# Loading x of four tiles in transfers of uneven row counts, in a kernel bound by its stores

## The chip, the cores and the metric

The kernel runs on one core of one Trainium2 chip. The metric is device time in microseconds (us), lower is better. The kernel before took 1336.84 us (median of 3 runs, 1336.64 to 1336.99). A ratio is the mean time of one kernel's fast runs over that of the other's of the same rounds, so it is not quite the ratio of the medians that are quoted beside it; the interval behind it is 95%. "Faster" and "slower" mean by more than 2%.

## The reference

```python
# r_inputs: (4096, 32, 64) float32; W: (496, 64, 64) float32, one matrix for each pair i < j of the 32 fields
i_idx, j_idx = np.triu_indices(32, k=1)
vdotw = einsum('bpd,pde->bpe', inputs[:, i_idx, :], W)
out = (vdotw * inputs[:, j_idx, :]).reshape(4096, 496 * 64)
```

The output has 4096 x 31744 floats, 520 MB, and must be written once. The inputs are 42 MB.

## The kernel before

The 4096 batch rows are 32 tiles of 128. TensorE transposes x of a tile and multiplies it by W (which stays in SBUF); VectorE multiplies the products in PSUM by x and writes them into a ring in SBUF; each tile leaves in four stores on SyncE's queue. x has three slots in SBUF and comes on ScalarE's queue, two tiles to a load.

```python
STORES = [[0, 1], [2, 3], [4, 5, 6], [7, 8, 9, 10, 11, 12, 13, 14, 15]]
RING = 28160                                   # floats per partition, for the stores' data
# x_slots: loads [0], [1,2], [4,3], [5,6], [8,7], ... two tiles each, three slots
    def load_x(load):
        at = sum(len(before) for before in x_loads[: x_loads.index(load)]) * P * F * D
        n = len(load) * F * D
        s = load[0][1]
        nc.scalar.dma_start(                   # 128 rows of 16384 bytes for two tiles
            out=xbuf[:, s * F * D : s * F * D + n],
            in_=x[at : at + P * n].rearrange("(p c) -> p c", p=P),
        )
# ...
    for t in range(NT):
        for load in x_loads:
            if min(load)[0] == t + 1:
                load_x(load)                   # a tile ahead
        for s, group in enumerate(STORES):
            if at + store_w[s] > RING:
                at = 0
            osb = ring[:, at : at + store_w[s]]
            # ... transposes, matmuls, and VectorE's products into osb ...
            nc.sync.dma_start(
                out=out[:, t * cols + o0 : t * cols + o0 + store_w[s]], in_=osb
            )
```

## Time and profile before

| | before |
|---|---|
| median time | 1336.84 us |
| span of the core in the profile, granted TensorE clock | 1335.1 us, 0.962 |
| TensorE, VectorE busy | 87%, 89% |
| VectorE's waits for stores | 102.6 us in 44 waits |
| moved | 562.87 MB at 422 GB/s |

The prediction below shows the busy shares, the DMA queues and the waits. These lines of the same page complete them: bytes, the summary of the chain of work that ended last, and two lines of the DMA issues (count, KB each, median us from issue to landing).

```profile
HBM read 41.94 MB, written 520.09 MB: 421 GB/s over the span
...
DMA 47%; DVE 38%; issue 9%; PE 5%; DVEq 0%; ACT 0%
...
out_dram<-ring SPq DMA_DIRECT2D x32, 4896.0 KB, 17.7
...
x<-in_x_dram ACTq DMA_DIRECT2D x15, 2048.0 KB, 20.4
```

The chain of last work is nearly half transfers, and the transfers are stores: 520 of the 562 MB. Everything that VectorE finishes has to find room in the ring, and room comes when a store has landed on the last of its DMA engines: the one issued at 418.46 landed at 436.7 on the median engine and at 440.28 on the last, and VectorE went on at 440.37. x is a small part of the traffic, but its rows pass through the same engines (from 419.4 us the fast ones have 1448 ns of store, 611 ns of x, and so on in turn), and it is these rows that the change hands out unevenly.

### The profile page before, as it was taken

To read this page: it belongs to the slowest core of one execution; us is meant where nothing else is said; L and a number is where in the kernel's file an instruction comes from. 1 tells how busy PE (TensorE), PEld (TensorE's weight loads), DVE (VectorE), ACT (ScalarE), POOL (GpSimd) and SP (SyncE) were. 2 spreads that over 40 slices of the span, in tenths; PEclk is the share of its full clock that TensorE was granted. 3 is DMA by queue.
4 is the path that set the end of the run, shared out by engine and by line. 5 is a ranking of instruction groups with operands and counts; after the bars stand their busy time and mean duration, and the time that the engine had idled before them with its cause. 6 is when DMAs were issued, how large, how long until landed. Compare 5 with 4: busy or idle time off the path is not lost.

```text
span 1335.1 us, 13080 instructions
## 1 busy us (share of the span) xinstructions
PE 1160.6 (87%) x5376; PEld 544.9 (41%) x5376; DVE 1183.4 (89%) x1376; ACT 66.1 (5%) x65; POOL 0.7 (0%) x6
## 2 busy tenths in 40 slices
PE   6998989989899898998989889798998979989893
PEld 3443334443344443444444444344443434354441
DVE  5998989989899898998989899898998989989894
ACT  0000000000000000000000000000000000000000
POOL 0000000000000000000000000000000000000000
PEclk9999999989899999998989999899999999989997
DMA  9999999999999999999999999999999999999998
GB/s 397 433 430 430 431 428 430 418 433 430 413 425 410 436 414 427 426 414 433 405 432 431 419 429 411 432 426 421 428 413 430 426 407 417 429 421 423 429 425 352
DMA packets 21659, 562.87 MB, mean 422 GB/s; under 512 B 2400, under 2 KB 2400, under 8 KB 2656
## 3 DMA queue, kind: packets, MB, share of 16 engines
q1 hardware_dynamic: 19152, 528.49, 92.8%
q10 hardware_dynamic: 2448, 33.56, 5.9%
q8 instruction: 42, 0.69, 0.2%
q14 instruction: 17, 0.14, 0.0%
HBM read 41.94 MB, written 520.09 MB: 421 GB/s over the span
## 4 chain that ended last, share of the span: by engine, by line
DMA 47%; DVE 38%; issue 9%; PE 5%; DVEq 0%; ACT 0%
DMA out_dram<-ring 46%; DVE ring L180 32%; DVE ring L188 5%; PE pring L170 5%; DMA x<-in_x_dram 1%; DVEq L180 0%; PE pring L130 0%; ACT xT L131 0%; DVEq L225 0%; DVEq L188 0%
## 5 line engine op out<-in xcount | busy, mean ns | idle before, releaser
L170 PE MATMUL pring<-w,xT 64*128 64x512 f32 (+4 forms) x4864 | 1098.4, 564 | 146.4 <-DVE ring L180 133.5
L180 DVE TENSOR_TENSOR ring<-pring,x 128x1024 f32<-128x1024 f32 (+3 forms) x1056 | 1104.1, 1108 | 131.4 <-DMA out_dram<-ring 102.6
L170 PEld LDWEIGHTS pring<-w,xT 64*128 64x128 f32 x4864 | 489.3, 191 | 711.7 <-DVE ring L180 533.0
L131 ACT COPY xT<-pring 128x1024 f32<-128x1024 f32 x64 | 64.8, 1012 | 1224.1 <-PE pring L130 1224.1
L188 DVE TENSOR_TENSOR ring<-pring,x 128x64 f32<-128x64 f32 (+3 forms) x320 | 97.7, 356 | 2.6 <-DMA out_dram<-ring 1.9
L130 PEld LDWEIGHTS pring<-ident,x 128*128 128x128 f32 x512 | 55.6, 142 | 58.8 <-DVE ring L180 50.2
L130 PE MATMUL pring<-ident,x 128*128 128x128 f32 x512 | 70.8, 282 | 8.6 <-DMA x<-in_x_dram 8.6
L131 ACT ACT_TABLE_LOAD x1 | 1.3, 1283 | 1.7 <-PEq L221 1.7
masks.py:199 POOL TENSOR_SCALAR_AFFINE_SELECT ident<-ident 128x128 f32<-128x128 f32 x1 | 0.3, 292 | 0.1
masks.py:197 POOL MEMSET ident<- 128x128 f32 x1 | 0.2, 204 | 0.3 <-POOLq L221 0.3
L221 POOL MEMSET const-bfloat16-1.0<- 128x1 bf16 x1 | 0.1, 101 | 0.0
L221 POOL MEMSET const-uint8-127<- 128x1 uint8 x1 | 0.1, 101 | 0.0
L221 POOL MEMSET const-float32-0.0<- 128x1 f32 x1 | 0.1, 98 | 0.2 <-issue 0.2
L221 POOL MEMSET const-float32-1.0<- 128x1 f32 x1 | 0.1, 98 | 0.0
## 6 DMA issues: line engine op xcount, KB each, us to landing
out_dram<-ring SPq DMA_DIRECT2D x32, 4896.0 KB, 17.7
out_dram<-ring SPq DMA_DIRECT2D x32, 3936.0 KB, 18.1
out_dram<-ring SPq DMA_DIRECT2D x32, 3776.0 KB, 18.3
out_dram<-ring SPq DMA_DIRECT2D x32, 3264.0 KB, 18.6
x<-in_x_dram ACTq DMA_DIRECT2D x15, 2048.0 KB, 20.4
w<-in_w_dram SPq DMA_DIRECT2D x1, 2592.0 KB, 28.1
x<-in_x_dram ACTq DMA_DIRECT2D x2, 1024.0 KB, 12.8
w<-in_w_dram SPq DMA_DIRECT2D x1, 2016.0 KB, 22.2
```

Source lines behind the costliest of these rows:

```text
L130: nc.tensor.transpose(pt[:, ts(c, P)], xt[:, ts(n * g + c, P)], ident)
L131: nc.scalar.copy(xT[:, ts(g, 2 * BANK)], pt)
L170: nc.tensor.matmul(pm[:, h * BANK : h * BANK + n], xT[h * D : (h + 1) * D, ts(p, P)], w_sb[h * D : (h + 1) * D, a : a + n], start=True, st ...
L180: nc.vector.tensor_tensor(runs(osb, o[0], o[1], n), runs(pm, 0, BANK, n), bass.AP(xj.tensor, xj.offset, [xj.ap[0], [0, 2], xj.ap[1]]), ALU ...
L188: nc.vector.tensor_tensor(osb[:, o[h] + h * D : o[h] + n], pm[:, h * (BANK + D) : h * BANK + n], xj[:, h * D :], ALU.mult,)
L221: nc = bacc.Bacc("TRN2", target_bir_lowering=False, num_devices=1)
```

## The change

Its intent, as described with it: 112 rows of x of four tiles come by the lowest seven DMA engines, so that the others are relieved. Each of the four loads concerned is issued per tile, and the tile named in `PART_LOADED` in five pieces of 16, 49, 49, 7 and 7 rows.

```diff
+PART_LOADED = [4, 12, 20, 28]
+ROWS = [slice(0, 16), slice(16, 65), slice(65, 114), slice(114, 121), slice(121, 128)]
...
-        nc.scalar.dma_start(
-            out=xbuf[:, s * F * D : s * F * D + n],
-            in_=x[at : at + P * n].rearrange("(p c) -> p c", p=P),
-        )
+        dst = xbuf[:, s * F * D : s * F * D + n]
+        src = x[at : at + P * n].rearrange("(p c) -> p c", p=P)
+        if not any(t in PART_LOADED for t, _ in load):
+            nc.scalar.dma_start(out=dst, in_=src)
+            return
+        for k, (t, _) in enumerate(load):
+            c = ts(k, F * D)
+            for r in ROWS if t in PART_LOADED else [slice(0, P)]:
+                nc.scalar.dma_start(out=dst[r, c], in_=src[r, c])
```

## The prediction

> **What bounds the kernel now.** I read the page's busy shares first, then the DMA queues, the waits, and the chain of work in one load period. The first lines:
>
> ```profile
> PE 1160.6 (87%) x5376; PEld 544.9 (41%) x5376; DVE 1183.4 (89%) x1376; ACT 66.1 (5%) x65; POOL 0.7 (0%) x6
> ...
> DMA  9999999999999999999999999999999999999998
> ...
> q1 hardware_dynamic: 19152, 528.49, 92.8%
> q10 hardware_dynamic: 2448, 33.56, 5.9%
> ```
>
> VectorE is busy 89% of the span of 1335.1 us, so it is not the limit. The packets of the four DMA queues add up to 92.8 + 5.9 + 0.2 = 98.9% of sixteen DMA engines' span (q1 carries the stores and w, q10 carries x). Sixteen equal engines at 98.9% would leave 1.1%, some 14.7 us, and that caps what balancing can bring, unless packets get quicker. The waits agree: VectorE's long waits are for stores that have not landed and whose ring space it wants.
>
> ```profile
> DVE ring L180 <- DMA out_dram<-ring: 102.6, 44, 6.2
> ```
>
> The share of sixteen hides which engine it is. Each transfer has sixteen landings in the trace, one an engine. I took them for all 128 stores. After 330 us the picture is the same everywhere: some twelve to fourteen land within 0.2 us of each other, one or two are up to 2 us late (mean of the second last: 1.6 us after the median), and one is 3.5 to 6.5 us late (mean of the last there: 4.3 us). It was 2.0 us on average in the first 165 us, then about 4. So one engine is behind the others all the time, and a store is finished when that one is.
>
> The packet records have no engine number, but a packet starts 3 or 4 ns before its predecessor on the engine ends, so they can be chained into engines. The chain that lands last has all its 133 + 17 transfers, 1329 us of packets after taking off the overlaps, and only 2.1 us in gaps over 60 ns. It is simply full. Its packets are longer: 992, 1142, 1199 and 1481 ns (medians for the 26112, 30208, 31488 and 39168 byte rows of a store), against 968, 1119, 1166 and 1448 ns in the chains of others. Eight rows of each a tile make 8 x (24 + 23 + 33 + 33) = 0.9 us a tile, 29 us in 32 tiles. Three chains of other engines, which came out complete, have 1313 us of packets, 8 of these in 39168-byte packets that were stretched (mean 1483 against 1448) just after a pause, and 14 to 15 us of gaps. They have 20 us or so to spare; the full one has nothing.
>
> Where the others pause is seen at a load, here the one of tiles 12 and 11, in two-microsecond windows (the last two columns are the share of sixteen DMA engines and GB/s):
>
> ```profile
> 415.00:417.00 2.00, 1.77 (x11) 1.18 (x12) 2.00 (x3) 0.00 (x0) 0.00 (x0) 1.00 1.14 488
> 417.00:419.00 2.00, 2.00 (x11) 1.43 (x11) 2.00 (x7) 0.00 (x0) 0.00 (x0) 1.00 0.23 99
> 419.00:421.00 2.00, 2.00 (x14) 1.34 (x12) 2.00 (x3) 0.00 (x0) 0.00 (x0) 1.00 1.03 325
> ```
>
> At 417.8 the fast engines run dry until the next store, issued at 418.46, reaches them at 419.37. The slow engine still works on the store before it until 423.1. The chain there:
>
> ```profile
> 418.46 21.82 DMA out_dram<-ring
> 440.28 0.03 issue
> ...
> 461.66 17.18 DMA out_dram<-ring
> ```
>
> That store lands at 440.28 on the slow engine (436.7 on the median one), VectorE gets its space and goes on at 440.37, and the next store of this kind is issued at 461.66. Here too the slow engine has work left, until 466.4. So it has 4 to 5 us in hand whenever the others starve: it never idles, and its own sum of packets is the time.
>
> [...] The trace agrees that exactly one engine is slow, and cannot say its number. [...] an engine alternates between its queues packet by packet. The trace agrees: from 419.4 us a fast engine does 1448 ns of store, 611 ns of x, 1448, 611, eight times.
>
> **The change part by part.** A normal load gives each engine eight rows of a tile. With 16, 49, 49, 7 and 7 rows, engines 0 to 6 get 1 + 7 + 7 + 1 + 1 = 17 rows and engines 7 to 15 get 1. The four loads concerned bring two tiles each. Before, a row of both tiles was one packet of 16384 bytes; after, it is two of 8192 bytes, as in the first and the last load (309 ns, against 611).
>
> - The slow engine, if it is among 7 to 15: removed 8 x 616 ns = 4.93 us (its mean for 16384 bytes); added 9 packets (8 of the normal tile, 1 of the other) x 311 ns = 2.80 us. Minus 2.13 us a load, minus 8.5 us in four. It lies on the path whole, since that engine has no gap.
> - Engines 0 to 6: 25 x 309 = 7.73 us in place of 8 x 611 = 4.89: plus 2.84 us a load, plus 11.4 us in four. They have about 20 us to spare, so it lies beside other work, as long as they don't fall behind the slow one by much. At a load after 330 us they are 3.7 us or more ahead; the shift between them is 2.84 + 2.13 = 4.97, so they come out about 1 us behind it, and are ahead again after one or two tiles at 0.9 us a tile. At the first load, of tiles 4 and 3 near 91 us, the slow engine is only 1.6 us behind, and engines 0 to 6 come out some 3 us behind it. They then set when space comes free, within the 4 to 5 us that the slow one has in hand. I allow 0.7 us for what of this shows.
> - Issues: five more on ScalarE's queue, at 0.37 us each some 2 us, four times. ScalarE is 5% busy and its next copy is 13 us later: nothing.
> - Semaphore writes are packets of 9 ns: nothing.
>
> Sum: 1336.84 - 8.5 + 0.7 = 1329.0 us.
>
> **The order of the two tiles, the step I doubted most.** In each of these loads the part-loaded tile (4, 12, 20, 28) goes out before its mate (3, 11, 19, 27), which is needed first. On engines 0 to 6 the mate's rows stand behind 17 packets, and each waits for a store's packet. If all were issued at 418.46, the 25th packet would come after eight rounds of 1448 + 309, eight of 1119 + 309 and eight of 968 + 309 ns, 35.7 us, and land at about 456; tile 11 is first transposed at 451.3. But the old single load waited for the later of two slots. ScalarE reaches it early:
>
> ```profile
> 409.15 1.01 ACT L131 COPY xT<-pring 128x1024 f32<-128x1024 f32 x1 [18.09 <-PE pring L130]
> 418.46 0.37 ACTq L106 DMA_DIRECT2D x<-in_x_dram  x1
> ```
>
> Tile 12's slot was tile 8's, done with some 40 us earlier, so its five transfers can go at 410. Eight of the 17 packets then travel with the store in flight and fill the pause at 417.8, eight with the next, and the mate's eight follow with the one after it: landing at about 447, some 4 us before it is needed (2 us if VectorE runs 2 us ahead). At 745.9 and 1074.1 us the gap from load to transpose is as long (33.0 and 33.8 us).
>
> [...]
>
> **The rivals.**
> - A: the mate's late x stalls TensorE, because the transfers don't go early. Against it: the two slots are tracked apart, for VectorE works on the third slot while a load is in flight. It would hold the store at 461.66 back by some 3 to 5 us, starve all engines, and eat the 2.1 us a load or more: 1336 to 1340.
> - B: the slow engine is among 0 to 6. Then it gets plus 2.84 us four times: 1336.84 + 11.4 = 1348. For it: no record has the number. Against it: [...] that the change was aimed this way. I give it 5%.
> - C: the spare time of engines 0 to 6 isn't usable where it is wanted (most of it lies after 250 us, in pauses), or their rows, which go to other engines' partitions, take longer than 309 ns. Then part of the 8.5 us is lost: 1330 to 1335.
>
> **Range and chances.** The gain can hardly exceed 8.5 us plus noise of 0.3 us or so[...]. So 1326.5 at the lower end. C and part of A make the upper end 1335. No mechanism here makes 2% (26.7 us): even balance without loss gives 14.7, and B costs 11.4.
>
> **What would show it right or wrong.** Right: mean DMA share still about 99% over a span 7 to 9 us shorter; VectorE's waits for stores shorter; the pause at 417 to 419 smaller; the last landing of a store less late behind the median just after each of the four loads by 2 to 3 us, with seven engines now late with it; no wait of TensorE for x beyond the first, of 8.6 us. Wrong: TensorE's transposes waiting for x in tiles 2, 10, 18 and 26 (A); stores after the four loads landing 3 us later than before, with one engine nearly 8 us behind (B); x rows of over 309 ns on a queue (C).

## The result and the profile after

The changed kernel took 1348.39 us (1348.32 to 1348.65, 6 runs) against 1336.90 us of the kernel before in the same rounds: ratio 1.0086 (1.0073 to 1.0099), "same" by the 2% rule, but 11.5 us longer where 7.8 us less were predicted. The results are correct.

The page of the changed kernel, first the lines that answer to the prediction's first ones (busy shares, DMA share in 40 slices, queues with packets, MB and share of sixteen engines), then the wait of VectorE for the stores (us in total, times, longest) and that of TensorE for x:

```profile
PE 1165.1 (87%) x5376; PEld 556.1 (41%) x5376; DVE 1183.7 (88%) x1376; ACT 66.1 (5%) x65; POOL 0.7 (0%) x6
...
DMA  9999999999998999999999999999999999999998
...
q1 hardware_dynamic: 19152, 528.49, 92.1%
q10 hardware_dynamic: 3136, 33.56, 5.9%
```

```profile
DVE ring L190 <- DMA out_dram<-ring: 108.0, 47, 6.2
...
PE pring L140 <- DMA x<-in_x_dram: 8.7, 1, 8.7
```

VectorE works as long as before (1183.7 against 1183.4 us). The DMA shares of the queues fell to 92.1 + 5.9 + 0.2 = 98.2%, over a span of 1346.5 us, which is 1322 us of packets for a mean engine; before it was 98.9% of 1335.1, or 1320 us. So the engines together do the same work, and nearly all of the longer span is idle time of some of them: balance got worse. TensorE never waits for x except at the very start, as before (8.6 us there). The granted clock in these two profiles, 0.962 and 0.953, is no cause: a longer run told below had 0.960.

Where it happens is seen at a load. The chain of work around tile 12's load, kernel after (start, length):

```profile
382.27 20.25 DMA out_dram<-ring
402.52 0.03 issue
...
411.72 20.63 DMA out_dram<-ring
432.35 0.03 issue
```

And the timeline of ScalarE there:

```profile
382.27 4.00 ACTq L119 DMA_DIRECT2D x<-in_x_dram  x5
393.32 1.01 ACT L141 COPY xT<-pring 128x1024 f32<-128x1024 f32 x1 [19.14 <-PE pring L140]
416.59 1.01 ACT L141 COPY xT<-pring 128x1024 f32<-128x1024 f32 x1 [22.26 <-PE pring L140]
426.31 0.38 ACTq L119 DMA_DIRECT2D x<-in_x_dram  x1
```

The five pieces go at 382.27, as soon as tile 8 has been read for the last time, and the mate, tile 11, alone at 426.31. The pieces go earlier than at the 410 of the prediction, so the mate did not stand behind them: it had landed on all engines by 443.1, and the first transpose of it came at 457.1.

For each transfer the trace has its landings, one an engine: sixteen, and seven for a 49-row piece. Each line gives those of one transfer in us after their median, in order (worked out from the trace, not a view):

```
49 rows, issued at 382.7:  -0.71 -0.66 -0.38  0.00  0.06  0.08  2.43
49 rows, issued at 383.0:  -0.70 -0.69 -0.38  0.00  0.03  0.09  2.43
store, issued at 391.1, the last eight:  0.04  3.90  3.91  4.23  4.59  4.63  4.68  8.68
store, issued at 398.5, the last seven:        3.61  3.66  3.96  4.32  4.36  4.40  8.30
store, issued at 426.3, the last four:   0.04  0.06  0.07  4.17
for comparison, before, store of 428.5, the last two:  1.72  3.66
```

Seven engines come late behind the others after the pieces, as they should. One of the seven is later than the other six by 4 us, which is just the distance at which the slow engine is always behind (4.17 two stores later, when the six have caught up). And one of the seven is already 2.4 us late with the 49-row pieces themselves. This speaks for a slow engine among the seven, to which the change gave rows instead of taking them; the chains of packets below show it.

Two-microsecond windows of before and after, where the engines other than the late ones run dry (third busy column: VectorE; last two columns: share of sixteen DMA engines, GB/s). Before, from 421 on, two microseconds after its pause at 417 to 419:

```profile
421.00:423.00 2.00, 2.00 (x12) 0.80 (x10) 1.82 (x2) 0.00 (x0) 0.00 (x0) 1.00 1.00 432
423.00:425.00 2.00, 1.00 (x5) 0.17 (x4) 0.70 (x1) 0.00 (x0) 0.00 (x0) 1.00 1.05 453
```

After:

```profile
411.00:413.00 2.00, 1.76 (x8) 0.30 (x4) 0.69 (x1) 0.00 (x0) 0.00 (x0) 1.00 1.04 435
413.00:415.00 2.00, 0.71 (x4) 0.30 (x4) 0.99 (x2) 0.00 (x0) 0.00 (x0) 1.00 0.92 393
...
421.00:423.00 2.00, 2.00 (x10) 0.87 (x12) 1.87 (x4) 0.00 (x0) 0.00 (x0) 1.00 0.52 220
423.00:425.00 2.00, 1.77 (x11) 1.03 (x10) 2.00 (x4) 0.00 (x0) 0.00 (x0) 1.00 0.44 189
425.00:427.00 2.00, 2.00 (x11) 1.56 (x11) 2.00 (x6) 0.00 (x0) 0.00 (x0) 1.00 0.30 130
```

Before, the pause at 417 to 419 (share 0.23, shown in the prediction) costs a mean engine 0.77 x 2 = 1.5 us, and by 421 all are busy. After, the six microseconds from 421 cost it (0.48 + 0.56 + 0.70) x 2 = 3.5 us. VectorE is busy in them; its wait lies before, at 411 to 415, where it stands 2.3 us until 414.0 for ring space, because the store of 391.1 landed on its last engine only at 413.9. So its next store is ready only at 426.3, and the engines that are done have nothing to move until then. The slow engine can't make up what it has lost, since it works through the pauses of the others already (before, its 1329 us of packets had 2.1 us of gaps).

The chains of packets say it too. Chained as in the prediction, exactly one chain of the kernel after has longer store packets than the rest (22 to 33 ns more in the median, by row size), and that chain has 241 packets of the x queue. An engine among the lowest seven should have 11 x 8 + 2 x 8 + 4 x (17 + 8) = 204 rows of x and one semaphore write for each of its 11 + 2 + 4 x 6 = 37 transfers, so 241; one of the other nine should have 88 + 16 + 4 x (1 + 8) = 140 rows and one write for each of its 11 + 2 + 4 x 2 = 21 transfers, so 161. The sum fits the page: 7 x 241 + 9 x 161 = 3136, the packets of q10; and the page's packets under 512 B, the semaphore writes, are 2576 against 2400 before, 176 more, as four times 60 in place of 16 should be. The slow chain is one of the seven.

The DMA issues of the kernel after, as a check that the pieces are what they should be (count, KB each, and for the second the median us to landing):

```profile
x<-in_x_dram ACTq DMA_DIRECT2D x8, 392.0 KB
...
x<-in_x_dram ACTq DMA_DIRECT2D x4, 128.0 KB, 6.5
x<-in_x_dram ACTq DMA_DIRECT2D x8, 56.0 KB
```

### The profile page after: what moved, and what is told of

Read it like the earlier page. It is cut to its first block, busy times and chain, and to the rows that moved or that the text cites. A ratio compares the mean times of both kernels' runs of the same rounds, so it can differ in the third digit from the quotient of the medians.

```text
span 1346.5 us, 13121 instructions
## 1 busy us (share of the span) xinstructions
PE 1165.1 (87%) x5376; PEld 556.1 (41%) x5376; DVE 1183.7 (88%) x1376; ACT 66.1 (5%) x65; POOL 0.7 (0%) x6
## 2 busy tenths in 40 slices
DMA packets 22348, 562.88 MB, mean 418 GB/s; under 512 B 2576, under 2 KB 2576, under 8 KB 2832
## 3 DMA queue, kind: packets, MB, share of 16 engines
q1 hardware_dynamic: 19152, 528.49, 92.1%
q10 hardware_dynamic: 3136, 33.56, 5.9%
## 4 chain that ended last, share of the span: by engine, by line
DMA 49%; DVE 33%; PE 10%; issue 7%; DVEq 0%; ACT 0%
DMA out_dram<-ring 48%; DVE ring L190 28%; PE pring L180 10%; DVE ring L198 5%; DMA x<-in_x_dram 1%; PE pring L140 0%; DVEq L190 0%; ACT xT L141 0%; DVEq L235 0%; DVEq L198 0%
## 5 line engine op out<-in xcount | busy, mean ns | idle before, releaser
L180 PEld LDWEIGHTS pring<-w,xT 64*128 64x128 f32 x4864 | 499.9, 193 | 712.0 <-DVE ring L190 523.8
```

The source lines that it names most:

```text
L180: nc.tensor.matmul(pm[:, h * BANK : h * BANK + n], xT[h * D : (h + 1) * D, ts(p, P)], w_sb[h * D : (h + 1) * D, a : a + n], start=True, st ...
```

## The experiments

The theory after the result: time is the sum of the slow engine's packets; the slow engine is one of the lowest seven; so each row of x more on it costs one packet, about 0.31 us, and each row fewer gains as much. Rivals: that the splitting itself costs the 11.5 us (more issues, more semaphores, smaller packets); that the heavy load on any seven engines costs it, slow or not; and that it is not an engine that is slow, but certain rows of the output.

On how many engines a piece goes is seen in the packets of q10, one for each row and one semaphore write for each engine of a transfer: the 3136 of the change, 3088 of low6 and 2720 of sw_skip come out with 16 engines for 16 rows, seven for 49 and for 7, ten for 10, six for 102, four for 4 and twelve for 24. Low4's piece of 68 rows has four landings. Which engines these are no trace shows: I assumed that k engines are always the lowest k, numbered from 0, and the shares in the diffs and the expectations are worked out so. Number 4 then stands for the engine that has a part in a piece of five engines and none in a piece of four. Only `ROWS` and `PART_LOADED` change unless a diff shows more; the diffs are against the kernel after. There were two batches of four runs on one chip, and a third of three runs on another (the results carry the chip numbers 12 and 11). Each batch had its own runs of the kernel before: 1336.72, 1336.86 and 1336.85 us. All results were correct.

**even5: five pieces, but eight rows to each engine.**

```diff
-ROWS = [slice(0, 16), slice(16, 65), slice(65, 114), slice(114, 121), slice(121, 128)]
+ROWS = [slice(0, 16), slice(16, 64), slice(64, 96), slice(96, 112), slice(112, 128)]
```

> Five transfers of 16, 48, 32, 16 and 16 rows for the same four tiles, as many as in the change and issued as early, but each on all sixteen engines: every engine keeps 8 rows. Theory 1 (the slow engine is among the lowest seven and the added packets are the loss): as before, within 1 us of 1336.9 (16 rather than 8 packets of x a load, 8 x 7 ns x 4, is 0.2 us). Theory 2 (the splitting costs: more transfers, semaphores that come round sooner, the mate behind its partner's rows): near the change's 1348, at least 1342.

Measured: 1338.37 us (1338.3 to 1338.53), ratio 1.0012 (0.9997 to 1.0027). It has as many issues as the change and an even share, and costs 1.65 us of the 11.5. So the splitting is not the cause. The 1.65 us, more than the 1 us that was allowed, are only partly explained: two packets of 313 ns in place of one of 616 on the slow engine, eight times in each of four loads, are 0.3 us.

**low4, low2 and low6: the same four tiles, with the heavy engines the lowest four, two or six.**

```diff
-ROWS = [slice(0, 16), slice(16, 65), slice(65, 114), slice(114, 121), slice(121, 128)]
+ROWS = [slice(0, 48), slice(48, 60), slice(60, 128)]   # low4: engines 0-3 21 rows, 4-11 4, 12-15 3
+ROWS = [slice(0, 80), slice(80, 94), slice(94, 128)]   # low2: engines 0-1 23 rows, 2-13 6, 14-15 5
+ROWS = [slice(0, 16), slice(16, 26), slice(26, 128)]   # low6: engines 0-5 19 rows, 6-9 2, 10-15 1
```

> 48 + 12 + 68 rows: engines 0 to 3 get 21 rows, 4 to 11 get 4, 12 to 15 get 3. Theory 1: if the slow engine is one of 0 to 3, 13 more rows x 0.31 us x 4 loads = 16 us more, 1353; if it is 4, 5 or 6, 4 rows fewer x 0.31 x 4 = 5 us less, 1332. In the first case one of the four landings of the 68-row transfer is 2 to 4 us behind the other three, in the second all four land together. Theory 2: near 1345 either way (three transfers rather than five).

> 80 + 14 + 34 rows: engines 0 and 1 get 23 rows, 2 to 13 get 6, 14 and 15 get 5. Theory 1: 15 x 0.31 x 4 = 18.6 us more (1355.5) if the slow engine is 0 or 1, 2.5 us less (1334.4) if it is 2 to 6. Theory 2: as low4.

> 16 + 10 + 102 rows: engines 0 to 5 get 19 rows, 6 to 9 get 2, the rest 1. Theory 1: 11 x 0.31 x 4 = 13.6 us more (1350.5) if the slow engine is 0 to 5, 7.4 us less (1329.5) if it is 6. Theory 2: as low4.

Measured: low4 1343.93 us (1343.47 to 1345.67), ratio 1.0056 (1.0041 to 1.0071); low2 1343.24 us (1341.01 to 1345.53, two of its runs near 1341 and two near 1345), ratio 1.0053 (1.0036 to 1.007); low6 1350.71 us (1350.7 to 1350.79), ratio 1.0104 (1.0089 to 1.0119).

low6 is clear. It puts 44 more rows on engines 0 to 5 and adds 14.0 us, while if the slow one had been number 6, it would have lost 24 rows. So it is one of 0 to 5. Its page:

```profile
q1 hardware_dynamic: 19152, 528.49, 92.0%
...
HBM read 41.94 MB, written 520.09 MB: 417 GB/s over the span
```

Its stores (q1) have 92.0% of a span of 1349.0 us, against 92.1% of 1346.5 after: the same 1240 to 1241 us of store packets in a longer span. Its clock was 0.960, close to that of the kernel before, so the clock doesn't make these kernels slow.

low4 and low2 were neither of the outcomes that the slow engine alone would give. With it among 0 to 3, low4 would have come out near 1353 us; without, well below the kernel before. Both came to 7 us over it, and I could not tell from the times which engine did that. The sign that was named for low4 in advance misled, too: one of the four landings of the 68-row piece of tile 12 was 3.15 us behind the other three, as expected for a slow engine among 0 to 3. The landings of the stores helped. When the last one is the slow engine, its lag grows inside a tile, as its longer packets add up; low6, the three first stores of tile 10, has 4.36, 4.60 and 4.86 us. In low4 the same stores have 4.77, 4.74 and 4.69: the last is an engine with normal packets that was given too many rows and catches up slowly. The chains agree: the one that lands last there has the normal 1448 ns a 39168-byte row. So there is a second limit: with 13 or 15 more rows in each of four loads, another engine than the slow one becomes the last. In low4 it is one of the four, about 3 us behind its three fellows; why it is behind them stays open.

**low5_two, low4_two and dose2: two of the four tiles only.** Half the dose was to keep an engine with normal packets from setting the time, so that the number of the slow one can be read from it.

```diff
-PART_LOADED = [4, 12, 20, 28]
+PART_LOADED = [12, 20]
+ROWS = [slice(0, 32), slice(32, 43), slice(43, 128)]   # low5_two: engines 0-4 20 rows, 5-10 3, 11-15 2
+ROWS = [slice(0, 48), slice(48, 60), slice(60, 128)]   # low4_two: as low4
                                                        # dose2: the rows of the change
```

> Only two tiles (12 and 20) in parts of 32 + 11 + 85 rows: engines 0 to 4 get 20 rows, 5 to 10 get 3, the rest 2. The runs before leave engines 4 and 5 for the slow one (low6: it is one of 0 to 5; low4: its four heavy engines were not the ones with long packets, and became the limit by their own added rows). If it is 4: 12 rows more x 0.31 us x 2 loads = 7.4 us more, 1344.2. If it is 5: 5 rows fewer x 0.31 x 2 = 3.1 us less, 1333.7.

> low4's rows (21 for engines 0 to 3, 4 or 3 for the rest) for two tiles in place of four. If low4 was slow because engines 0 to 3 ran out of spare time (a second limit near 1326 plus 16 us) while the slow engine, 4 or 5, was relieved: 4 x 0.31 x 2 = 2.5 us less, 1334.3, and the heavy ones come to some 1326 + 8 = 1334, so 1333.5 to 1336. If the slow engine is one of 0 to 3 after all: 13 x 0.31 x 2 = 8 us more, 1345. If low4's 7 us were half a cost of splitting: 1340.

> The change itself (16, 49, 49, 7, 7 rows) for tiles 12 and 20 only. If each such load costs the slow engine's 17 - 8 = 9 rows: half of the change's 11.5 us, 1342.6. If the early load of tile 4, when all engines are full, is the costly one: under 1340.

Measured: low5_two 1344.56 us (1344.34 to 1344.9), ratio 1.0058 (1.0043 to 1.0073); low4_two 1336.32 us (1335.8 to 1337.19), ratio 0.9997 (0.9982 to 1.0012); dose2 1342.85 us (1342.68 to 1342.98), ratio 1.0045 (1.0028 to 1.0061).

dose2 has half the rows and half the loss, 6.0 us against 11.5. low5_two loads the lowest five with 24 rows in all and loses 7.7 us; low4_two loads the lowest four with 26 and loses nothing, where 1345 us would have been the time with the slow engine among them. (1333.5 to 1336 us had been expected; it came out 0.3 us above that.) So the slow engine is number 4, the fifth lowest. In low5_two, too, exactly one chain has the longer store packets, and the traces show without the times on which side it is: in low6 that chain has 27 packets of 8192 bytes at the load of tile 20, the 19 + 8 of a heavy engine; in low4_two, at the load of tile 12, it has 10 in the parts that could be chained, of the 4 + 8 of a light engine, where a heavy one has 21 + 8.

**halves: each store as two transfers of 64 rows** (against the kernel before). It was meant to give the engines other rows of each store, to tell a slow engine from slow rows; that it does was assumed, not shown.

```diff
-            nc.sync.dma_start(
-                out=out[:, t * cols + o0 : t * cols + o0 + store_w[s]], in_=osb
-            )
+            for r in (slice(0, 64), slice(64, 128)):
+                nc.sync.dma_start(
+                    out=out[r, t * cols + o0 : t * cols + o0 + store_w[s]], in_=osb[r]
+                )
```

> The kernel before, with each store as two transfers of 64 rows. Each engine then moves four rows of either half[...]. If the long packets belong to an engine: still one engine with 33 ns more a packet in all windows, and 1337 (0 to 3 us more for 128 more issues). If they belong to rows (of memory or partitions): the long packets are shared out over two or more engines, the fullest has half the excess, and the time falls by some 10 us, to 1326 to 1330.

Measured: 1887.5 us (1884.31 to 1898.35), ratio 1.4133 (1.409 to 1.4176). That is 550 us over the kernel before, neither of the two outcomes expected, and inconclusive for its question. Its page:

```profile
DMA packets 23708, 562.89 MB, mean 299 GB/s; under 512 B 4448, under 2 KB 4448, under 8 KB 4704
```

and, from the waits, VectorE's for the stores:

```profile
DVE ring L180 <- DMA out_dram<-ring: 472.5, 76, 12.5
```

The same bytes move at 299 instead of 422 GB/s, and VectorE waits for stores 472.5 us instead of 102.6. It is no lack of issued work: the packets of the stores still fill 92.6% of the longer span, so each takes longer: 92.6% of sixteen spans of 1884.1 us over q1's 17024 rows of stores and w are 1.64 us a row, against 1.16 us before (92.8% of sixteen spans of 1335.1 us; estimates from the pages). What makes a packet of a 64-row transfer longer is not shown by any run.

**pad_low5: low5_two with every row of the output 4352 bytes longer in memory**, cut off on the host by indexing. If certain rows of the output in memory were slow, this moves them.

```diff
+PAD = 1024 + 64
-    NT = out.shape[1] * 2 // (F * (F - 1) * D)
+    NT = (out.shape[1] - PAD) * 2 // (F * (F - 1) * D)
-    ... (P, NT * NP * D), F32, kind="ExternalOutput")
+    ... (P, NT * NP * D + PAD), F32, kind="ExternalOutput")
-    return r.results[0]["out_0_dram"].reshape(B, NP * D)
+    return r.results[0]["out_0_dram"][:, : NT * NP * D].reshape(B, NP * D)
```

> low5_two with each output row 4352 bytes longer in memory (the surplus is cut off on the host), so every row of the output lies at another address and at another distance from its neighbours. If the long packets belong to the engine: as low5_two, 1344 to 1345, one engine with 33 ns more a packet. If they come from where that engine's rows lie in memory: the long packets go to another engine or go away, and the time leaves 1344.6: 1330 to 1334 if the engine is then above the five heavy ones or if none is slow.

Measured: 1344.68 us (1344.46 to 1344.88), ratio 1.0059 (1.0045 to 1.0072), on the other chip. low5_two had 1344.56. So where the rows lie in memory, at least by this much of a shift, does not matter, and it is on this chip too one of the lowest five that is slow.

**low4_mild: a version meant to be faster.** Seven tiles, and only three rows more on engines 0 to 3, one fewer on the others, number 4 among them.

```diff
-PART_LOADED = [4, 12, 20, 28]
-ROWS = [slice(0, 16), slice(16, 65), slice(65, 114), slice(114, 121), slice(121, 128)]
+PART_LOADED = [4, 8, 12, 16, 20, 24, 28]
+ROWS = [slice(0, 112), slice(112, 116), slice(116, 120), slice(120, 124), slice(124, 128)]
```

> A version meant to gain: 112 + 4 + 4 + 4 + 4 rows for seven tiles (4, 8, ... 28). Engines 0 to 3 get 11 rows, all others 7. If the slow engine is number 4 it sheds 7 x 0.31 = 2.2 us: 1334.7; engines 0 to 3 get 3 x 0.31 x 7 = 6.5 us more on a limit that low4 puts at 1343.9 - 16.1 = 1328, so 1334.5: just in balance, 1334.5 to 1336. If the slow engine is one of 0 to 3: 1343.4.

Measured, in 5 rounds: 1335.71 us (1335.53 to 1335.98) against 1336.85 us (1336.51 to 1337.11), ratio 0.9992 (0.9979 to 1.0004). The single runs do not overlap, and the medians differ by 1.1 us; the interval of the ratio includes 1. It is the fastest version, and a gain of a thousandth. It also places the slow engine on this second chip: had it been one of 0 to 3, it would have got 21 more rows, some 6.5 us. With pad_low5, it is number 4 there too. The trace agrees: the chain with the long packets has 15 packets of 8192 bytes at the load of tile 28, the 7 + 8 of a light engine; one of 0 to 3 would have 19. VectorE's wait for stores is what it was before:

```profile
DVE ring L190 <- DMA out_dram<-ring: 102.9, 43, 6.2
```

**sw_skip: 88 rows of the four tiles on GpSimd's queue, to steer round number 4.** The hope was that none of the 88 rows would go by number 4. That was my guess, without a measurement behind it; it would have left number 4 two rows in place of eight, 6 x 0.31 x 4 = 7.4 us less, 1329.4 us by estimate.

```diff
-ROWS = [slice(0, 16), slice(16, 65), slice(65, 114), slice(114, 121), slice(121, 128)]
+ROWS = [slice(88, 92), slice(92, 96), slice(96, 100), slice(100, 104), slice(104, 128)]
+    skip = const.tile([5, 8], F32, tag="skip", name="skip")
...
+            if t in PART_LOADED:
+                nc.gpsimd.dma_start(out=skip[:, :], in_=x[0:40].rearrange("(p c) -> p c", p=5))
+                nc.gpsimd.dma_start(out=dst[0:88, c], in_=src[0:88, c])
```

> A version meant to gain more: in the four tiles 88 rows are loaded from GpSimd's queue, after a dummy transfer of five rows of 32 bytes from the same queue, the rest as 4 + 4 + 4 + 4 + 24 rows as before from ScalarE. [...] If 88 rows are spread over 15 or 16 engines: engine 4 keeps 8 rows, 1336 to 1338. [...]

Measured, in 5 rounds: 1338.11 us (1338.02 to 1338.42), ratio 1.001 (0.9996 to 1.0023): no gain. In the view of the DMA queues and issues:

```profile
q0 software_dynamic: 576, 2.89, 0.6%
...
x<-in_x_dram POOLq DMA_DIRECT2D x4, 704.0 KB, 17.9
```

The queue carried the 4 x 88 rows, 2.89 MB. The chains show them at six to an engine on nearly every engine in each load, and each transfer has sixteen landings. Number 4 kept 6 + 2 = 8 rows, as in an even load. This is the case of 15 or 16 engines, for which 1336 to 1338 us were expected (it came out 0.1 us above).

Together, rows of x added to engine 4 and the time over the kernel before of the same rounds:

| run | rows added to number 4 | time added |
|---|---|---|
| low6 | 4 x 11 = 44 | 14.0 us |
| the change | 4 x 9 = 36 | 11.5 us |
| low5_two | 2 x 12 = 24 | 7.7 us |
| pad_low5 | 2 x 12 = 24 | 7.8 us |
| dose2 | 2 x 9 = 18 | 6.0 us |
| low4_two | 2 x (-4) = -8 | -0.5 us |
| low4_mild | 7 x (-1) = -7 | -1.1 us |

The five additions cost 0.32 to 0.33 us a row, the length of one 8192-byte packet (0.31) and a little. From dose2 to low6 it is 8.0 us for 26 rows, 0.31 a row, so some 0.4 us of each addition belongs to something else, the splitting perhaps. The subtractions gain less than a packet each; in these runs engines 0 to 3 were near the end themselves, by the estimate that follows.

How near can be estimated from the runs in which they were the last: low4 gave them 4 x 13 = 52 rows, 16.1 us at 0.31, and took 1343.93, so without these rows they would be done at 1327.8; low2 gave 60, 18.6 us, so 1324.6; low4_two gave 26, 8.1 us, so 1328.3, if they were the last there. That is 8.5 to 12 us ahead of the kernel before, not 20, for the last of them.

## Why the prediction was wrong

**What bounds the kernel: right.** One engine is slow, it has no gap, and its sum of packets is the time. The five additions in the table follow one line. That rows taken from it gain as much is not shown: seven fewer gained 1.1 us.

**The step that failed: "The slow engine, if it is among 7 to 15".** It is number 4, among the engines to which the change gives rows. With this the sum is that of rival B: "Then it gets plus 2.84 us four times: 1336.84 + 11.4 = 1348", and 1348.39 us were measured. The mechanism and the size of B were right, and 5% was its chance. With the slow engine's own packets (a mean of 313 ns in the pieces; 616 before), the term is 25 x 0.313 - 8 x 0.616 = 2.90 us, four times 11.6 us. For choosing the other I had nothing measured: I took it for evidence that the change was aimed this way, which says nothing about where the engine is. The trace before had no number for it, as the prediction said. That was a reason for an even chance, or for two answers side by side; not for 19 to 1.

**"They have about 20 us to spare": mis-sized.** The runs show 8.5 to 12 us, for the last of engines 0 to 3. So even with the slow engine among 7 to 15, the other half of the sum would have failed: that engine done at 1324.6 to 1328.3, plus 11.4, is about 1336 to 1340 us (an estimate from the runs above). By this estimate the predicted gain of 8.5 us was not to be had by this set of rows. The gaps that I had counted, 14 to 15 us, and the excess of stretched packets, 8 us, came from three chains whose numbers are not known, and low4 shows one of 0 to 3 about 3 us behind its fellows. Also, they were perhaps not all free for rows; no run separates that.

**"Tile 12's slot was tile 8's ... so its five transfers can go at 410": the reason was right, the time wrong.** They went at 382.27, a tile earlier. The mate was in time in all four loads; rival A didn't happen, and TensorE's only wait for x is the first one. Of C, the half on longer rows fell: the median in the pieces is 309 ns on the others and on the slow engine too (means 310 and 313). Its other half, that the spare time can't be used, is what the estimate above points to.

**Issues and semaphores: nearly right.** They showed nothing in the profile of the change: its trace has eight semaphores for the transfers, as before, and when one was used again its last transfer had landed at least 9.9 us earlier (21.6 us in the kernel before; worked out from the traces). But even5, which has them all with an even share, costs 1.65 us, of which I can explain 0.3.

**What would show it wrong, said in advance, was what came.** "Stores after the four loads landing 3 us later than before, with one engine nearly 8 us behind (B)": the store at 391.1 had its last landing 8.68 us behind the median.

**What stays open.** Why number 4 is slow. Its excess is 22 to 33 ns in a store's packets, but small in the loads of x: means of 313 against 310 ns in the pieces (17 rows of a tile in place of its usual eight, so at least nine of them to other partitions), and 616 against 613 ns in its usual rows. Neither the place of the output in memory nor the chip changed it. But which partitions of SBUF an engine reads for a store is in no trace; they may be the same each time, and halves, which was to part the two, could not: whether the engine is slow, or reading certain partitions, is not shown. One core on each of two chips is little, too. That low4_mild gains 1.1 us and not 7 packets' worth (2.2) I put down to engines 0 to 3 being nearly full, which is argued from the estimate above and not shown.

## What to carry to other kernels

When one member of a set sets the time, find out which one it is before giving it less to do; the sharing of the load is one experiment with half of the members loaded and half not, and a change that is aimed at the wrong half can cost more than was hoped for (here 11.5 us, for 8.5). A share of busy time over sixteen engines does not show it (here 98.9% before, 98.2% after); the landings of one transfer, engine by engine, do (here the last 3.5 to 6.5 us behind the median), and nested sets of heavy engines name it, here in five runs. Before moving work to those that "have time", load them in one run and see when they become the last.
